# Routed experts on one core: gate and up products of the next tile of places ahead of the down product of this one

## The chip, the cores and the metric

The kernel runs on one core of one Trainium2 chip. The metric is the device time of one execution in microseconds, and the median over the runs is compared. A core has five engines that work side by side, each on its own queue of instructions: TensorE (PE, with its weight loads shown as PEld), VectorE (DVE), ScalarE (ACT), GpSimd (POOL) and SyncE (SP). Here SP only issues loads and stores. POOL issues the scatters and computes small things.

## The reference

The input is x of 32 x 256 x 128 floats, that is T = 8192 tokens of 128 numbers. Two layers follow one another, and each has the form x + s * silu(g). In layer 0, s is a two-layer transformer with rotary attention and g is a mixture of 64 small experts. In layer 1, s is a linear attention with 16 heads of 8 numbers, and g is the part that the change touches:

```python
    x = hidden_states.reshape(-1, h)
    shared_out = _swiglu(x, shared_gate_w, shared_up_w, shared_down_w)
    logits = x @ gate_w
    topk_ids = jnp.argmax(logits, axis=-1)
    topk_val = jnp.max(logits, axis=-1)
    scores = jax.nn.sigmoid(topk_val)[:, None]
    xs = x * scores
    ...
    g = _grouped_mm(sorted_x, routed_gate_w, tokens_per_expert)
    u = _grouped_mm(sorted_x, routed_up_w, tokens_per_expert)
    d = _grouped_mm(jax.nn.silu(g) * u, routed_down_w, tokens_per_expert)
```

Each token goes to one of 32 experts. The expert multiplies it by a gate matrix and an up matrix (128 x 256 each), takes silu(gate) * up, and multiplies the result by a down matrix (256 x 128). Everything is in float32.

## The kernel before, in words

One function, `recurrent_kernel`, does both layers. Its last third is layer 1, and only that matters here. A tile is 128 tokens (or places), and a group is GT = 4 tiles.

*Sending.* Tokens are sorted by expert without a sort: every expert owns a whole number of tiles of 128 places, 96 tiles (S1) in all, and every token has a place. `send()` (L858) scatters the token rows from `s_rows` into the DRAM buffer `xslot`, one indirect DMA of POOL per tile of tokens.

*Routed experts.* `routed()` (L959) walks over 24 groups of 4 tiles of places. For a group it loads `e_x` from `xslot` (L963, two buffers), transposes it on PE (L132, into a PSUM bank `ps_tr`), and copies it to `e_xt` on ACT (L973). DVE makes the destination rows `e_toi` from the last column of `e_x` (L969 to L971). Then, for each of the four tiles:

- SP reads the tile's expert from `widx` and loads its three weight matrices as `e_w` (L983, 384 KB, six buffers);
- PE multiplies four 128 x 128 pieces into one PSUM bank `ps_sc` (L986): the two halves of the gate and of the up product. This is "the gate/up product" below;
- ACT takes the Silu of the gate half into `e_hs` (L991, three buffers), and DVE multiplies it by the up half (L992);
- PE multiplies `e_hs` by the down matrix in two pieces (L995), into half of a PSUM bank `ps_mm` (two buffers, shared with other work). This is "the down product";
- ACT copies it to `e_ys` (L999), and POOL scatters `e_ys` to the rows of `back` (L1000).

*Linear attention.* `linear_attention(g)` (L873) works on 4 tiles of tokens at a time, for 16 groups. It is beside the routed experts until the last group. Its steps on PE are L877 (queries), L885 (norms of queries), L895 (keys and values), L924 (states), L936 (queries times states), a transpose of `l_o` (L132), and L952 (output). DVE has a long chain for it: L911, L915, L916 (a reciprocal), L917, and after L936 the steps L938, four pairs L109/L110 (mean and variance) and L116. Between the last two stands a chain on POOL (L111, L112, L114: `bn_rs`). ACT takes a square root in each group (L914), for which another function table is loaded, and the Silu table again after it.

*The finish.* `finish(g)` (L1011) loads `back`, adds the shared expert's part by two products with the identity (L1021, L1022), takes Silu, multiplies by the attention and adds x. It waits for the scatters.

*What sets the order.* The functions are Python generators: at each `yield` another one goes on (`run`, `rolling`), and this gives the order in which the instructions are written down. The tile framework then places them at build time: it gives each instruction the priority of its place, keeps a clock from a cost table for every engine, and takes from the ready instructions the first. So the order on an engine is close to the written one but not equal to it; the gate/up product of a later tile stands ahead of the down product of an earlier one wherever the planner found the latter not yet ready. On the chip every engine takes its queue in exactly the order so fixed, and waits on semaphores.

Of the kernel before, what the change touches and what calls it, by code (L numbers as in the profile page):

```python
# [16 lines left out]
F32 = mybir.dt.float32  # L17
I32 = mybir.dt.int32
U32 = mybir.dt.uint32
AF = mybir.ActivationFunctionType  # L20
ALU = mybir.AluOpType
# [4 lines left out]
P = 128  # L26
BATCH, SEQ, D = 32, 256, 128
T = BATCH * SEQ
NT = T // P
GT = 4  # L30
# [4 lines left out]
E1, F1 = 32, 256  # L35
# [25 lines left out]
def recurrent_kernel(ctx: ExitStack, tc: tile.TileContext, x, consts, small0, wsd, wgu, wd, small1, bias1, wr, out):  # L61
    nc = tc.nc
    vec, act, pool, pe, sp = nc.vector, nc.scalar, nc.gpsimd, nc.tensor, nc.sync
# [9 lines left out]
    def bank(tag="mm", bufs=2):  # L73
        return psum.tile([P, GW], F32, tag=tag, name=f"ps_{tag}", bufs=bufs)
# [6 lines left out]
    back = dram.tile([T + S1 * P, D], F32, name="back")  # L81
    moe1 = dram.tile([T, D], F32, name="moe1")

    def rows(ap, g):
        return ap[g * GW : (g + 1) * GW].rearrange("(t p) d -> p t d", p=P)
# [42 lines left out]
    def transposed(src):  # L128

        ps = bank("tr", 2)  # L130
        for j in range(GT):
            pe.transpose(ps[:, j * P : (j + 1) * P], src[:, j], ident)  # L132
        return ps
# [175 lines left out]
    with ExitStack() as c0:  # L309
# [3 lines left out]
        wk = c0.enter_context(tc.tile_pool(name="wk0", bufs=2, side="right"))  # L313
# [489 lines left out]
    wk = ctx.enter_context(tc.tile_pool(name="wk1", bufs=2))  # L803
# [20 lines left out]
    widx = w1p.tile([1, S1], I32, name="widx")  # L824
# [10 lines left out]
    owner = w1p.tile([S1, 1], F32, name="owner")  # L835
# [5 lines left out]
    ps = bank()  # L841
# [14 lines left out]
    sent, returned, last_norm = [], [], []  # L856
# [101 lines left out]

    def routed():  # L959

        for i in range(S1 // GT):
            xg = wk.tile([P, GT, D + 1], F32, name="e_x", bufs=2)
            ins = sp.dma_start(xg, rows(xslot, i))  # L963
            for d in sent[-8:]:
                tc.add_manual_dep(ins.ins, d.ins.name, waits, reason="reads what all the scatters wrote")
            ps = transposed(xg[:, :, :D])
            to = wk.tile([P, GT], F32, name="e_to")
            toi = wk.tile([P, GT], I32, name="e_toi", bufs=6)
            vec.tensor_scalar(to, xg[:, :, D], 0.0, None, ALU.is_equal)  # L969
            vec.tensor_tensor(to, to, spare[:, i * GT : (i + 1) * GT], ALU.mult)  # L970
            vec.scalar_tensor_tensor(toi, to, -1.0, xg[:, :, D], ALU.add, ALU.add)  # L971
            xt = works[1].tile([P, GW], F32, tag="chan", name="e_xt")
            act.copy(xt, ps)  # L973
            ys = works[1].tile([P, GT, D], F32, tag="out", name="e_ys")
            yield
            for j in range(GT):
                wt = wk.tile([P, 3 * F1], F32, name="e_w", bufs=6)
                at = i * GT + j
                row = nc.values_load(
                    widx[:, at : at + 1], engines={mybir.EngineType.SP}, min_val=0, max_val=(E1 - 1) * P,  # L980
                    skip_runtime_bounds_check_because="the owner is held at E1 - 1",
                )
                sp.dma_start(wt, wr[bass.ds(row, P)])  # L983
                ps = bank("sc", 4)
                for c in range(4):
                    pe.matmul(  # L986
                        ps[:, c * P : (c + 1) * P], wt[:, c * P : (c + 1) * P], xt[:, j * P : (j + 1) * P],
                        start=True, stop=True,
                    )
                hs = wk.tile([P, F1], F32, name="e_hs", bufs=3)  # L990
                act.activation(hs, ps[:, :F1], AF.Silu)  # L991
                vec.tensor_tensor(hs, hs, ps[:, F1:], ALU.mult)  # L992
                yp = bank()
                for c in range(2):
                    pe.matmul(  # L995
                        yp[:, :D], hs[:, c * P : (c + 1) * P], wt[:, 2 * F1 + c * D : 2 * F1 + (c + 1) * D],
                        start=c == 0, stop=c == 1,
                    )
                act.copy(ys[:, j], yp[:, :D])  # L999
                ins = pool.indirect_dma_start(  # L1000
                    out=back, out_offset=bass.IndirectOffsetOnAxis(ap=toi[:, j : j + 1], axis=0),
                    in_=ys[:, j], in_offset=None,
                )

                if returned:
                    tc.declare_no_dep(ins.ins, group="returned", reason="the rows are disjoint")
                tc.add_to_no_dep_group("returned", ins.ins)
                returned.append(ins)
                yield

    def finish(g):  # L1011

        tl = slice(g * GT, (g + 1) * GT)
        tag = ("gate", "tok", "chan", "out")[g % 4]
        gr = work(g // 4 + g).tile([P, GT, D], F32, tag=tag, name="f_g")
        ins = sp.dma_start(gr, rows(back, g))
        for d in returned[-8:]:
            tc.add_manual_dep(ins.ins, d.ins.name, waits, reason="reads what all the scatters wrote")

        ps = bank("sc", 4)  # L1020
        pe.matmul(ps, ident, xt_at[g], start=True, stop=False)  # L1021
        pe.matmul(ps, ident, gr.rearrange("p t d -> p (t d)"), start=False, stop=True)  # L1022
        act.activation(gr, ps.rearrange("p (t d) -> p t d", d=D), AF.Silu)
        yield
        vec.tensor_tensor(gr, gr, s_all[:, tl], ALU.mult)
        vec.tensor_tensor(gr, gr, x_at[g], ALU.add)
        sp.dma_start(rows(out, g), gr)
        yield

    sending, routing = send(), routed()  # L1030
    attending = rolling([linear_attention(g) for g in range(NG - 1)], 3)
    while len(sent) < NT:
# [94 lines left out]
```

## Time and profile before

| what | value |
|---|---|
| median of 3 runs | 1350.44 us (1348.21 to 1351.1) |
| the profiled execution | 1348.85 us |
| its span, first to last instruction | 1347.1 us |
| PE busy over the span | 1226.4 us (91%) |
| DVE, ACT, POOL busy | 940.0, 785.7, 650.4 us |
| mean granted clock of PE | 0.972 |
| gate/up products (L986), first and last start | 1050.6 and 1299.8 us |
| down products (L995), first and last start | 1054.9 and 1301.6 us |

A row of the profile's groups or of its timeline names engine, line, operation, the tile written and the tiles read. A float32 product of 128 columns shows as two passes, so one tile's gate/up product is x8 and its down product x4. A bracket such as `[0.74 <-DVE e_hs L992]` says how long the engine stood still before that row and whose end released it. A matmul's end is modelled: rows overlap, and eight passes advance PE by 0.89 us where each is shown longer.

### The profile page before, as it was taken

What the parts mean: (1) busy time and instruction counts of PE and PEld (TensorE: products, weight loads), DVE (VectorE), ACT (ScalarE), POOL (GpSimd) and SP (SyncE); (2) the same over time, 40 slices, a digit from 0 to 9 for tenths busy, and PEclk for the clock granted to TensorE, in tenths of its full rate; (3) what the DMA queues carried; (4) which work ended last, traced back from release to release, by engine and by line L of the source; (5) the groups of instructions that cost most, each with busy time, mean ns of one, the idle gap of its engine ahead of it and who ended that gap; (6) DMA issues with size and microseconds to landing.
All of it is one profiled execution on the core that took longest, in us unless ns stands there. A gap on an engine that the chain in (4) does not pass through costs nothing. (4 is left out here: it accounts for less than half of the span.)

```text
span 1347.1 us, 22826 instructions
## 1 busy us (share of the span) xinstructions
PE 1226.4 (91%) x7425; PEld 864.0 (64%) x7425; DVE 940.0 (70%) x3064; ACT 785.7 (58%) x1858; POOL 650.4 (48%) x1020
## 2 busy tenths in 40 slices
PE   6989999999999799999997978899999899999797
PEld 4547576576566477667665645566566778788773
DVE  4699779879879746655664866667767666666437
ACT  1785665675676576766775766353545555545342
POOL 6362822732721656665736365442677243443440
PEclk9999999999999999999998988889989899999999
DMA  5020301301302232223201142411211556666667
GB/s 181 22 55 25 118 17 47 118 25 40 102 25 81 69 81 55 57 57 74 59 7 39 42 116 63 124 32 55 93 44 46 172 185 209 203 200 199 185 210 201
DMA packets 135079, 125.80 MB, mean 93 GB/s; under 512 B 17104, under 2 KB 110256, under 8 KB 134832
## 3 DMA queue, kind: packets, MB, share of 16 engines
q1 hardware_dynamic: 123696, 108.57, 27.0%
q0 software_dynamic: 11264, 15.78, 4.8%
q8 instruction: 59, 0.97, 0.3%
q14 instruction: 60, 0.49, 0.1%
HBM read 83.63 MB, written 40.68 MB: 92 GB/s over the span
## 5 line engine op out<-in xcount | busy, mean ns | idle before, releaser
L1000 POOL DMA_INDIRECT back<-e_ys,e_toi x96 | 96.3, 1003 | 129.3 <-ACT e_ys L999 104.5
L601 ACT ACTIVATE a_pr<-ps_sc,a_nm 128x256 f32<-128x256 f32 x256 | 119.1, 478 | 59.2 <-DVE a_nm L592 59.1
L663 PE MATMUL ps_mm<-xt,sw 128*128 128x512 f32 x256 | 134.1, 630 | 1.6 <-ACT e_y L523 0.9
L111 POOL TENSOR_SCALAR bn_rs<-bn_mv 128x4 f32<-128x4 f32 x112 | 28.7, 256 | 218.5 <-DVE bn_mv L110 191.1
L125 POOL TENSOR_SCALAR z<-s_rows,bn_rs 128x128 f32<-128x128 f32 x256 | 128.4, 521 | 6.6
L681 PE MATMUL ps_mm<-sw,m_h 128*128 128x128 f32 x1024 | 127.9, 279 | 2.3 <-ACT e_y L523 1.3
L681 PEld LDWEIGHTS ps_mm<-sw,m_h 128*128 128x128 f32 x1024 | 119.6, 192 | 12.8 <-issue 6.0
L668 DVE SCALAR_TENSOR_TENSOR m_h<-m_h,m_z 128x512 f32<-128x512 f32 x128 | 89.5, 703 | 46.0 <-ACT m_h L667 45.3
L112 POOL TENSOR_TENSOR bn_rs<-bn_rs,power 128x4 f32<-128x4 f32 x112 | 116.7, 1043 | 1.3
L592 DVE TENSOR_REDUCE a_nm<-ps_sc 128x2 f32<-128x512 f32 x128 | 83.3, 679 | 31.9 <-PE ps_sc L586 31.7
L986 PE MATMUL ps_sc<-e_xt,e_w 128*128 128x128 f32 x768 | 101.4, 278 | 2.9 <-ACT e_xt L973 2.9
L665 ACT ACTIVATE m_z<-ps_mm,fold 128x512 f32<-128x512 f32 x128 | 87.3, 685 | 28.3 <-PE ps_mm L663 27.9
L986 PEld LDWEIGHTS ps_sc<-e_xt,e_w 128*128 128x128 f32 x768 | 94.3, 194 | 9.3 <-ACT e_xt L973 4.9
L586 PE MATMUL ps_sc<-a_qk,a_qk 64*128 64x256 f32 x512 | 96.7, 412 | 1.2 <-ACT a_pr L601 1.1
L524 POOL DMA_INDIRECT sums<-e_y,sidx x32 | 51.1, 1598 | 80.5 <-ACT e_y L523 39.5
L618 PE MATMUL ps_tr<-con,a_pr 128*128 128x128 f32 x512 | 75.9, 278 | 9.4 <-ACT a_pt L619 5.5
L618 PEld LDWEIGHTS ps_tr<-con,a_pr 128*128 128x128 f32 x512 | 59.3, 143 | 37.8 <-issue 19.3
L667 ACT ACTIVATE m_h<-m_z 128x512 f32<-128x512 f32 x128 | 80.8, 635 | 1.7
L860 POOL DMA_INDIRECT xslot<-s_rows,dest x64 | 68.3, 1067 | 24.1 <-issue 18.5
L619 ACT COPY a_pt<-ps_tr 128x512 f32<-128x512 f32 x128 | 71.7, 590 | 12.8 <-PE ps_tr L618 11.7
L558 PE MATMUL ps_mm<-xt,sw 128*128 128x512 f32 x128 | 69.0, 645 | 6.5 <-ACT xt L546 2.7
L627 PE MATMUL ps_mm<-a_pt,a_v 128*64 128x256 f32 x512 | 70.9, 396 | 4.2 <-ACT m_z L665 3.5
(236 smaller groups left out, 2951.1 us busy)
## 6 DMA issues: line engine op xcount, KB each, us to landing
e_w<-in_wr_dram SPq DMA_DIRECT2D x96, 384.0 KB, 3.8
xslot<-zero SPq DMA_DIRECT2D x4, 1548.0 KB, 7.0
e_x<-xslot SPq DMA_DIRECT2D x24, 258.0 KB, 4.0
e_wg<-in_wgu_dram SPq DMA_DIRECT2D x16, 384.0 KB, 3.2
x_in<-in_x_dram SPq DMA_DIRECT2D x16, 256.0 KB, 3.7
tab<-s_rows SPq DMA_DIRECT2D x16, 256.0 KB, 2.4
sums<-s_y SPq DMA_DIRECT2D x16, 256.0 KB, 2.3
sums<-zero SPq DMA_DIRECT2D x4, 1024.0 KB, 8.4
```

What stands on the lines that cost most here:

```text
L112: pool.tensor_tensor(rs[:, 0], rs[:, 0], power, ALU.pow)
L125: ins = pool.tensor_scalar(dst[:, j], src[:, j], rs[:, 1, j : j + 1], rs[:, 0, j : j + 1], ALU.add, ALU.mult)
L586: pe.matmul(sc[h][:, j * SEQ : (j + 1) * SEQ], qk[0][hd, q0 : q0 + P], qk[1][hd, b * SEQ : (b + 1) * SEQ], start=True, stop=True,)
L592: vec.tensor_reduce(nm[:, 2 * h : 2 * h + 2], sc[h].rearrange("p (j k) -> p j k", k=SEQ), AX.X, ALU.max, negate=True)
L601: act.activation(pr[:, n], sc[h][:, j * SEQ : (j + 1) * SEQ], AF.Exp, bias=nm[:, n : n + 1], accum_out=su[:, n : n + 1],)
L618: pe.transpose(pts[:, n * P : (n + 1) * P], pr[:, n, k * P : (k + 1) * P], ident)
L663: pe.matmul(ps, par("w1", l * FF0 + f * P, P), xt, start=True, stop=True)
L665: act.activation(z, ps, AF.Identity, bias=fold[:, l, 3 + f : 4 + f])
L668: vec.scalar_tensor_tensor(h, h, 1.0, z, ALU.add, ALU.mult)
L681: pe.matmul(ps[:, j * D : (j + 1) * D], hs[f][:, j * P : (j + 1) * P], par("w2", l * FF0 + f * D, D), start=f == 0, stop=f == 3,)
L986: pe.matmul(ps[:, c * P : (c + 1) * P], wt[:, c * P : (c + 1) * P], xt[:, j * P : (j + 1) * P], start=True, stop=True,)
L1000: ins = pool.indirect_dma_start(out=back, out_offset=bass.IndirectOffsetOnAxis(ap=toi[:, j : j + 1], axis=0), in_=ys[:, j], in_offset=None,)
```

## The change

The body of the tile loop is split into two functions. `widened` loads the weights, multiplies gate and up, and takes silu and product; `returns` multiplies by the down matrix, copies and scatters. The loop calls `widened` for a tile and then `returns` for the tile before it, across the border of a group too. After the last tile `returns` is called once more. The operations and their counts are the same; only the place of `returns` in the written order moves by one tile.

```diff
+        def widened(at, xt):
+            wt = wk.tile([P, 3 * F1], F32, name="e_w", bufs=6)
...
+            sp.dma_start(wt, wr[bass.ds(row, P)])
+            ps = bank("sc", 4)
+            for c in range(4):
+                pe.matmul(ps[:, c * P : (c + 1) * P], wt[:, c * P : (c + 1) * P], xt, start=True, stop=True)
+            hs = wk.tile([P, F1], F32, name="e_hs", bufs=3)
+            act.activation(hs, ps[:, :F1], AF.Silu)
+            vec.tensor_tensor(hs, hs, ps[:, F1:], ALU.mult)
+            return wt, hs
+
+        def returns(wt, hs, ys, to):
+            yp = bank()
+            for c in range(2):
+                pe.matmul(
+                    yp[:, :D], hs[:, c * P : (c + 1) * P], wt[:, 2 * F1 + c * D : 2 * F1 + (c + 1) * D],
+                    start=c == 0, stop=c == 1,
+                )
+            act.copy(ys, yp[:, :D])
+            ins = pool.indirect_dma_start(
+                out=back, out_offset=bass.IndirectOffsetOnAxis(ap=to, axis=0), in_=ys, in_offset=None,
+            )
...
+        behind = None
         for i in range(S1 // GT):
...
             for j in range(GT):
-                wt = wk.tile([P, 3 * F1], F32, name="e_w", bufs=6)
-                at = i * GT + j
...
-                hs = wk.tile([P, F1], F32, name="e_hs", bufs=3)
-                act.activation(hs, ps[:, :F1], AF.Silu)
-                vec.tensor_tensor(hs, hs, ps[:, F1:], ALU.mult)
-                yp = bank()
...
-                yield
+                ahead = widened(i * GT + j, xt[:, j * P : (j + 1) * P])
+                if behind:
+                    returns(*behind)
+                behind = (*ahead, ys[:, j], toi[:, j : j + 1])
+                yield
+        returns(*behind)
+        yield
```

In the built programs, with the planner's order, both kernels have the same work on every engine: the same products on PE, and the same 34 loads of a function table on ACT. Lines of the changed kernel are numbered differently: the gate/up product is L972 there, Silu L974, the product with the up half L975, the down product L982, the copy L986, the scatter L987, the weight load L969, and for a group L999 (load of `e_x`), L1005 to L1007 (destinations) and L1009 (copy to `e_xt`).

More of the change, by code (lines that the diff above doesn't have):

```diff
@@ L959, in routed @@
     def routed():
+        def widened(at, xt):
+            wt = wk.tile([P, 3 * F1], F32, name="e_w", bufs=6)
+            row = nc.values_load(
+                widx[:, at : at + 1], engines={mybir.EngineType.SP}, min_val=0, max_val=(E1 - 1) * P,
+                skip_runtime_bounds_check_because="the owner is held at E1 - 1",
+            )
[17 more added lines that the diff above has]
+                out=back, out_offset=bass.IndirectOffsetOnAxis(ap=to, axis=0), in_=ys, in_offset=None,
+            )
+            if returned:
+                tc.declare_no_dep(ins.ins, group="returned", reason="the rows are disjoint")
+            tc.add_to_no_dep_group("returned", ins.ins)
+            returned.append(ins)
+        behind = None
         for i in range(S1 // GT):
@@ L976, in routed @@
             for j in range(GT):
-                wt = wk.tile([P, 3 * F1], F32, name="e_w", bufs=6)
-                at = i * GT + j
[L979 to L989, printed above, removed]
-                hs = wk.tile([P, F1], F32, name="e_hs", bufs=3)
-                act.activation(hs, ps[:, :F1], AF.Silu)
-                vec.tensor_tensor(hs, hs, ps[:, F1:], ALU.mult)
-                yp = bank()
[L994 to L1008, printed above, removed]
+                ahead = widened(i * GT + j, xt[:, j * P : (j + 1) * P])
+                if behind:
+                    returns(*behind)
+                behind = (*ahead, ys[:, j], toi[:, j : j + 1])
                 yield
+        returns(*behind)
+        yield
     def finish(g):
```

## The prediction

> **What bounds the kernel now.** I read first the slices of the page, then a table of stretches, to find the stage that the change touches and what fills it. It runs from the first gate/up product (1050.6 us) to the last down product (1301.6 us).
>
> ```profile
> PE   6989999999999799999997978899999899999797
> ...
> sum 253.00, PE 234.25 PEld 204.92 DVE 146.36 ACT 129.22 POOL 109.85; mean PE 46.85 PEld 40.98 DVE 29.27 ACT 25.84 POOL 21.97
> ```
>
> The sum is over 1050 to 1303 us. PE is busy for 234.25 of 253 us and no other engine for over 147. The change takes no work from PE, so what can be won is at most PE's idle time, 253 - 234.25 = 18.75 us, 1.4% of the whole. The second view is the waits of that stretch (waiting instruction, releaser, us in total, times, longest), those of PE and two of DVE:
>
> ```profile
> DVE e_hs L992 <- ACT e_hs L991: 40.6, 42, 2.6
> ...
> DVE e_to L969 <- DMA e_x<-xslot: 12.3, 12, 2.2
> ...
> PE ps_mm L995 <- DVE e_hs L992: 9.6, 15, 1.6
> ...
> PE ps_tr L132 <- DVE l_o L116: 4.8, 2, 2.7
> ...
> PE ps_sc L986 <- ACT e_xt L973: 2.9, 5, 1.5
> ...
> PE ps_mm L995 <- DVE l_n L888: 1.0, 2, 0.5
> ```
>
> PE's four make 18.3 us, so they are the whole idle time. Half of it, 9.6 us, is what the change goes for: the down product waits for its `e_hs`. The third view, the timeline, shows why it waits where the wait is long:
>
> ```profile
> 1097.57 1.28 ACT L991 ACT_TABLE_LOAD   x1
> 1097.72 0.17 DVE L969 TENSOR_SCALAR e_to<-e_x 128x4 f32<-128x4 f32 x1 [1.13 <-DMA e_x<-xslot]
> 1098.86 0.95 ACT L991 ACTIVATE e_hs<-ps_sc 128x256 f32<-128x256 f32 x3
> 1099.97 1.35 DVE L916 RECIPROCAL l_n<-l_n 128x192 f32<-128x192 f32 x1
> 1101.23 1.02 DVE L992 TENSOR_TENSOR e_hs<-e_hs,ps_sc 128x256 f32<-128x256 f32 x3
> 1101.65 1.16 PE L995 MATMUL ps_mm<-e_w,e_hs 128*128 128x128 f32 x8 [1.36 <-DVE e_hs L992]
> ```
>
> The first Silu was done at about 1099.2, but DVE took the product only at 1101.23: it had stood behind the load of `e_x` and then had the attention's chain to do. So a long wait is DVE's queue, not the length of gate, silu, product, down.
>
> **The change part by part.** *Nothing is added or removed*: by the instruction order of the two built programs, both have 384 matmuls of gate/up, 192 of down, and 34 table loads. What moves is the down product with its copy and its scatter.
>
> *Cover.* I call cover the PE work that stands between the end of a tile's gate/up product and its down product, added up in each program's order with the advance per instruction that the timeline shows (0.223 us a 128 x 128 product, 0.112 a transpose, 0.86 a 512-wide one). The cover needed with nothing in the way is 1.11 us (gate/up advanced to 1109.46, down at 1110.57). Before, the median of the 96 tiles is 1.74 us and 10 are under 1.1; after, 2.68 us and 3. The planner had already put a later gate/up product ahead nearly everywhere. What 1.11 us lacks sums to 2.2 us before and 0.3 after: that is the certain part, 1.9 us. In the last 16 tiles, without attention beside them, the cover goes only from 1.01-1.12 to 1.01-1.34.
>
> *The waits, place by place.* For the rest I walked the after order at each place where PE waits before, with durations from this trace (Silu 0.38, product 0.42, L916 1.26, four L109/L110 1.6, L116 0.3 for the first, POOL's chain 1.6 from L111 to the end of L114, `e_x` 4.2 from issue to landing).
>
> (a) `e_to` stands ahead of an `e_hs` on DVE and waits for `e_x`: 1143.10, 1154.93, 1165.94, 1287.62, waits 0.74 + 0.62 + 0.30 + 0.72 = 2.38. From the transposes that free the buffer to the down product behind, PE work is 4.17, 4.55, 4.84, 4.68; with the wait added, about 5.15 is needed. After: 4.84, 4.77, 5.73, 5.47, so 0.3 at the first; the second is reached late, through (d). 2.38 becomes 0.3.
>
> (b) The place above and its twin 1224.68 (1.36 + 1.55 = 2.91). After, the means L109/L110 go ahead of the wait for `e_x`, but L116 comes in before `e_hs`, and PE has 5.47 instead of 6.25 from freeing to down. Walk: issue and landing 4.25, L915 to L916 1.8, L116 0.5 (it waits for POOL), product 0.4: 7.0 against PE at 5.8. 2 x 1.2, and 0.15 each for `e_xt`: 2.7.
>
> (c) The groups of tiles 24 to 27 and 68 to 71 (waits at 1125.94, 1131.74 and 1250.11), where, after, L938 to L916 go ahead of the second `e_hs`: before 0.23 + 0.54 + 1.37 = 2.14. After, counted from the transposes of `e_x`: ACT is through root and second table load at 6.65 and through Silu at 7.0, DVE through L916 at 8.1 and the product at 8.5, and PE is there at 7.0: 1.6 twice, and 0.3 for L888: 3.5. A loss.
>
> (d) `e_xt`: 1149.57 (1.52), 1173.83 (0.66) and three of 0.20 to 0.24, 2.86. At the first, nothing lay between transposes and product before; after, 1.48 us does, and the 1.52 goes. But in the same group L916 (3.6 us after L936) goes ahead of an `e_hs` that PE wants at 2.8: 1.3. The others stay: 2.64.
>
> (e) `l_o` transposed: 2.67 + 2.12 = 4.79. At the first, POOL's `bn_rs` stood behind a scatter whose down product came late; after, that scatter is of tiles finished before L936, and the 2.67 goes. At the second, PE has 2.7 us of work from L936 to the transpose instead of 4.0, and the chain takes 4.9 with one scatter ahead: 2.3, and 0.5 behind it. 2.8.
>
> (f) Waits of 0.18 to 0.49: 1.66 before. After 0 but for a down product right behind L936 (0.5, twice): 1.0. The first wait (0.99) stands, the one for L888 at 1180.07 (0.49) falls to 0.2.
>
> Sum before 0.99 + 2.38 + 2.91 + 2.14 + 2.86 + 4.79 + 1.66 + 0.49 = 18.2. After 0.99 + 0.3 + 2.7 + 3.5 + 2.64 + 2.8 + 1.0 + 0.2 = 14.1. The walk goes only to places that wait before; a new order has others, for which I put 1.0 (four of the size of (f)). Gain 18.2 - 15.1 = 3.1 us. Its bounds: a gain of 18.3, all idle time, and a loss of 5.1, worked out under *slower*.
>
> *What else moves.* The copy and scatter follow the down product: copies wait 81.3 us in total on PE already, POOL is 43% busy here, and nobody needs a row of `back` before the finish. The last down product still comes right behind the last gate/up product, so the finish starts as before. The weight load of tile n+6 waits on SP for down product n. From there to its gate/up product is 4.24 us of PE work at least before and 5.13 after; issue to landing takes 3.8 us (median, 5.0 at most), and no gate/up product waits for weights before: no cost. `e_x` loads stand at the same place of SP's queue or at most two weight loads later.
>
> [...] The waits in (b), (c), (d) lie behind a pair of table loads. In the trace, table load to root to table load to Silu is 1095.89 to 1098.86, 2.97 us. [...] In the trace PE stood 1.36 us with ready products behind the waiting one: 3.1 stays.
>
> **The rivals.** *Nothing*: the planner had done it; the waits that remain are DVE's, and (c) and (d) give back what (a) and (e) win: 1350.4. For: the cover of 86 tiles was enough. Against: (e)'s 2.67 us hangs on one scatter's place.
>
> *All of it*: cover lets DVE be late everywhere: 9.6 us of `e_hs` and 1.0 of L888 go, (c) and (d) don't come: 1341. Against: at (b) cover is smaller after.
>
> *Slower*, by one mechanism: DVE's attention chain now goes ahead of `e_hs`, from L938 to L916 and in places L116. From L936 it takes about 4.0 us, and PE has 2.8 to 3.6 us of other work. Were this paid in all nine groups at 1.5 us, 13.5 us would stand against the 8 us that my sum has for such waits ((b), (c), 1.3 in (d), 1.0 in (f)): 5.5 more, 2.4 over the gain, 1352.8; and with 0.3 of L116 in each, 2.7 more, 1355.5. It decides from where `e_x` lands over 4.7 us after its issue (4.3 is the median here, 5.4 the longest) or POOL's `bn_rs` comes later than L916.
>
> **How the numbers follow.** 3.1 us off the span of 1347.1 gives 1344.0, the profiled execution 1345.7 instead of 1348.85; the median of the runs lies 1.6 us above that execution: 1347.3. Chances: this case 45% (own range 1344.5 to 1349.5), nothing 20%, slower 20%, all of it 15%. The range goes half into the last two: 1342 to 1353.5. 0.2%, 2.7 us, is about what these runs can tell apart (their spread is 2.9). Faster by more, below 1347.7: all of it and 27 of the 45: 0.42. Slower by more: 0.22. Between: 0.36.
>
> **What would show it.** Right: PE idle in this stage of about 15 us; waits of the down product on `e_hs` of about 7 us, with the longest at (c); no wait of 2.7 us on L116 near the 13th attention group, one of about 2.3 near the 14th; DVE's waits on `e_x` under 12.3. Wrong: gate/up waiting for `e_w`; down waits that appear in every group behind L916; a longer stretch from the last down product to the end.

## The result, and the profile after

The changed kernel takes 1337.55 us (median of 6 runs, 1331.24 to 1343.91) against 1351.36 us before (6 runs, 1348.21 to 1354.09). The ratio is 0.9895, with a 95% interval of 0.9877 to 0.9914: 13.8 us or 1.05% faster, where 3.1 us were forecast. It lies outside the range, below its low end of 1342.

The profiled execution took 1336.66 us. I split the span of both at the first gate/up product and at the last down product, by the starts of these rows:

| part, us | before | after | difference |
|---|---|---|---|
| before the stage | 1050.8 | 1053.9 | +3.1 |
| stage: first gate/up start to last down start | 250.9 | 237.1 | -13.8 |
| last down start to the end | 45.4 | 43.8 | -1.6 |
| span | 1347.1 | 1334.9 | -12.2 |

The gain lies in the stage. The part ahead of it is the same work in both kernels and still differs by 3.1 us between these two executions, so it is partly luck that the stage and the medians give the same 13.8 us. First the page of after (PE's 40 slices):

```profile
span 1334.9 us, 22827 instructions
...
PE   6989999999999899999998877889999899999997
```

Now the table of stretches, cut to the stage alone in each kernel. The columns are the length and the busy time of each engine.

```profile
sum 251.50, PE 232.75 PEld 204.41 DVE 145.66 ACT 129.18 POOL 109.05; mean PE 232.75 PEld 204.41 DVE 145.66 ACT 129.18 POOL 109.05
```
```profile
sum 237.90, PE 226.44 PEld 201.02 DVE 148.29 ACT 130.53 POOL 108.51; mean PE 226.44 PEld 201.02 DVE 148.29 ACT 130.53 POOL 108.51
```

PE's idle time falls from 18.75 to 11.46 us, 7.3 less. But its *busy* time falls too, by 6.3 us, although the products are the same in number and size and the granted clock was 0.99 and 1.00. A busy time that shrinks with no work taken away held something other than work.

So I counted anew, from start to start. In the trace the pass of a 128-column product begins 0.111 us after the one before it where nothing holds it (transposes 0.109, 512 columns 0.429). By these advances the stage has 216.3 us of PE work in both kernels. All beyond it is time by which matmuls start late: 34.6 us before, 20.8 us after. The rows hide the difference to the idle time, because a row of 128 columns is shown 0.275 us long and ends 0.164 us after the next could have begun.

| late time in the stage, us | before | after | difference |
|---|---|---|---|
| idle, as the rows show it | 18.75 | 11.46 | -7.3 |
| hidden in gaps over 0.2 us, behind the shown end of a matmul | 4.5 | 2.6 | -1.9 |
| gaps of up to 0.2 us, wholly hidden | 11.3 | 6.7 | -4.6 |
| sum | 34.6 | 20.8 | -13.8 |
| of it ahead of down products | 20.0 | 11.3 | -8.7 |
| ahead of gate/up products | 7.0 | 4.1 | -2.8 |
| ahead of transposes of `l_o` | 5.3 | 3.1 | -2.2 |

The waits of after, the answer to the list in the prediction (waiting instruction, releaser, us in total, times, longest):

```profile
DVE e_hs L975 <- ACT e_hs L974: 44.2, 54, 2.3
...
PE ps_mm L982 <- DVE e_hs L975: 6.9, 8, 1.1
...
DVE e_to L1005 <- DMA e_x<-xslot: 5.4, 6, 1.8
...
PE ps_tr L132 <- DVE l_o L116: 2.5, 3, 1.4
...
PE ps_tr L132 <- DMA e_x<-xslot: 1.0, 2, 0.8
...
PE ps_sc L972 <- ACT e_xt L1009: 0.6, 2, 0.4
```

Down products wait 6.9 us instead of 9.6, the layer norm's `l_o` costs 2.5 us instead of 4.8. DVE's wait for `e_x` falls from 12.3 to 5.4 us. New is 1.0 us of PE for `e_x` itself, near the end.

The timeline of after at the place that the prediction's third view showed:

```profile
1099.52 1.28 ACT L974 ACT_TABLE_LOAD   x1
...
1100.66 0.17 DVE L1005 TENSOR_SCALAR e_to<-e_x 128x4 f32<-128x4 f32 x1 [0.33 <-DMA e_x<-xslot]
...
1100.82 0.39 ACT L974 ACTIVATE e_hs<-ps_sc 128x256 f32<-128x256 f32 x1
...
1101.09 1.35 DVE L916 RECIPROCAL l_n<-l_n 128x192 f32<-128x192 f32 x1
...
1102.90 1.08 DVE L975 TENSOR_TENSOR e_hs<-e_hs,ps_sc 128x256 f32<-128x256 f32 x3
...
1103.13 0.30 PE L132 MATMUL ps_tr<-con,l_o 128*128 128x128 f32 x1 [0.53 <-DVE l_o L116]
...
1103.36 0.71 PE L982 MATMUL ps_mm<-e_w,e_hs 128*128 128x128 f32 x4
```

DVE still comes late to the product: the chain with L916 stands ahead of it as before. But PE has other work to do, and loses 0.53 us here instead of 1.36.

### The profile page after: what moved, and what is told of

The parts are those of the page before. It is cut to its first block, busy times and chain, and to the rows that moved or that the text cites. A ratio compares the mean times of both kernels' runs of the same rounds, so it can differ in the third digit from the quotient of the medians.

```text
span 1334.9 us, 22827 instructions
## 1 busy us (share of the span) xinstructions
PE 1222.2 (92%) x7425; PEld 863.2 (65%) x7425; DVE 943.5 (71%) x3064; ACT 787.6 (59%) x1858; POOL 650.6 (49%) x1020
## 5 line engine op out<-in xcount | busy, mean ns | idle before, releaser
L987 POOL DMA_INDIRECT back<-e_ys,e_toi x96 | 95.1, 991 | 106.3 <-ACT e_ys L986 73.2
L111 POOL TENSOR_SCALAR bn_rs<-bn_mv 128x4 f32<-128x4 f32 x112 | 27.9, 249 | 230.4 <-DVE bn_mv L110 207.0
L972 PE MATMUL ps_sc<-e_xt,e_w 128*128 128x128 f32 x768 | 100.8, 278 | 1.0 <-ACT e_xt L1009 0.6
L972 PEld LDWEIGHTS ps_sc<-e_xt,e_w 128*128 128x128 f32 x768 | 94.5, 194 | 9.8 <-issue 7.8
```

What stands on the lines that cost most here:

```text
L972: pe.matmul(ps[:, c * P : (c + 1) * P], wt[:, c * P : (c + 1) * P], xt, start=True, stop=True)
L987: ins = pool.indirect_dma_start(out=back, out_offset=bass.IndirectOffsetOnAxis(ap=to, axis=0), in_=ys, in_offset=None,)
```

## The experiments

Three theories were set against one another. *Theory 1*: PE loses the time at down products whose `e_hs` comes just in time or late, everywhere in the stage and half of it unseen in the rows; the cover takes it away. *Theory 2*: the gain comes from attention's chain, whose instructions the new order puts earlier on DVE and POOL. The steps from group to group spoke for it: from group 18 to 19 before took 17.8 us and after 10.6. *Theory 3*: the small gaps come from the weight load, since `e_hs` is the stationary operand and can't be loaded before it is finished.

Chips differ: the kernel before took 1349.4, 1366.3, 1367.0 and 1349.7 us on the four chips used here. Each result is therefore given as the ratio to runs of the kernel before on the same chip; stage times and late time come from the profiled execution of each.

### The down product without its wait

```diff
-                        yp[:, :D], hs[:, c * P : (c + 1) * P], wt[...],
+                        yp[:, :D], ident, wt[...],
```

> The kernel before, with one edit: the down product takes a constant tile as its stationary operand in place of e_hs, so its result is not the routed expert's. Silu and the multiply still run and write e_hs, but TensorE never waits for it; TensorE's passes are the same in number and size. Theory 1 (TensorE loses the time in many small waits for an e_hs that comes just in time, half of them hidden in the rows' busy time; counted from start to start of matmuls the down product's rows of before are 20.0 us late in sum): all of that goes, the stage from the first gate/up product to the last down product falls from 251 us to about 231 to 234 us, the time to 1330 to 1335 us. Theory 2 (the gain of the change came from attention's chain of VectorE and GpSimd being ordered earlier, and the waits for e_hs only stand where another wait would take over): the stage stays over 243 us, the time over 1344 us. Step as predicted (only 9.6 us of waits for e_hs can be won, and most of them come back elsewhere): 1341 to 1347 us.

Measured: 1329.99 us, ratio 0.9852 (0.9824 to 0.9879). The stage takes 232.2 us; down products are late by 4.0 us in sum instead of 20.0. The waits of PE in the stage:

```profile
PE ps_tr L132 <- DVE l_o L116: 4.2, 3, 2.5
PE ps_mm L995 <- DVE l_n L888: 1.2, 2, 0.6
PE ps_sc L895 <- DVE e_hs L992: 0.4, 1, 0.4
PE ps_sc L986 <- ACT e_xt L973: 0.4, 1, 0.4
```

This is what theory 1 said: what the waits for `e_hs` cost in the kernel before is about 19 us, not 9.6, and little comes back elsewhere. The late time of the whole stage falls from 34.6 to 16.7 us. PE's busy time in the stage is 226.5 us here, 6.3 less than before; up to 0.9 us of this is a 512-column product of the finish, which comes behind the last down product in this run. One caution: the planner knows of the missing wait and sets down products earlier, so this run isn't the old order without its waits. The change doesn't win a share of just this: ahead of down products it won 8.7 us where this run won 16.0, and it won 2.2 us ahead of the transposes of `l_o`, which are no better here (5.8 us late, 5.3 before).

### Half of the change

```diff
+                if i > 11 or (i == 11 and j == GT - 1):   # the second run: if i < 12
+                    returns(*behind)
+                    behind = None
```

> The change in groups 0 to 11 alone; in groups 12 to 23 each tile's down product follows its own gate/up product as before. Theory 1 (many small waits for e_hs, everywhere): the first twelve groups take about 127 us as in the changed kernel (133.8 before), the last twelve about 117 us as before; the time is 1343 to 1346 us. Theory 2 (attention's chain at one place, from group 18 to 19, where the changed kernel gained 7.1 us): no more than the first half's 6.4 us can show, and if it comes from attention's order rather than from the cover, it shows less than 3 us: 1347 to 1351 us.

> The change in groups 12 to 23 alone, the first twelve as before. Theory 1: the first twelve groups take about 134 us as before, the last twelve about 110 us as in the changed kernel (117.1 before), the time is 1342 to 1345 us, and what this and the run with the first half gain add up to the whole gain of 13 to 14 us. Theory 2 (one place, group 18 to 19): the step from group 18 to 19 takes 10 to 11 us instead of 17.8 and the time is 1338 to 1343 us, with all of the gain in that one group.

| us | ratio to before (95%) | groups 0 to 11 | groups 12 to 23 | late in group 18 |
|---|---|---|---|---|
| before | 1 | 133.8 | 117.1 | 7.2 |
| first half linked | 0.9951 (0.9933 to 0.9970) | 127.8 | 116.2 | 6.5 |
| second half linked | 0.9943 (0.9923 to 0.9963) | 136.2 | 110.8 | 0.4 |
| changed kernel | 0.9895 (0.9877 to 0.9914) | 127.4 | 109.7 | 0.5 |

By the ratios the halves gain 6.6 and 7.7 us, which add up to 14.3: the whole. Each half gains where it is linked. The order of the matmuls in groups 0 to 11 of the second run is that of before, and yet it took 136.2 us there instead of 133.8: one execution is good to some 2.4 us in a half, no better. Both theories hold a part. In the first half no transpose of `l_o` was late before, and the gain is spread: in the first run late time falls there from 15.8 to 9.9 us, by 4.0 ahead of down products and 2.8 ahead of gate/up products, and 0.9 is lost elsewhere. That is what cover would do; but attention's order changes with it, and no run parts the two there. In the second half nearly all of the gain stands in one group, 18.

### The change at one place

> The change in groups 16 to 19 alone, elsewhere as before. In group 18 matmuls are 7.2 us late in sum before and 0.5 us in the changed kernel, among them two waits for l_o (2.8 us in group 18, 2.3 us in group 19). Theory 2 for this place (one scatter less ahead of the layer norm's chain on GpSimd, one wait for l_o gone): 5 to 7 us, the time is 1342.5 to 1345 us and one of the two long waits for l_o is left. Theory 1 (cover alone, evenly in all groups): one sixth of the change's gain, 2.3 us, 1346.5 to 1348 us.

Measured: ratio 0.9945 (0.9928 to 0.9961), 7.5 us on a chip with 1366.34 us before. Group 18 is late by 0.4 us instead of 7.2, and one wait for `l_o` is left. In this profiled execution groups 16 to 19 are late by 7.0 us less than in the trace of before, but the other groups, which keep the old way, by 3.6 more; no trace of before was kept on this chip, so whether the chip or the execution does that is open. Theory 2 holds at this place, and the two timelines show how. POOL before, around the 13th attention group:

```profile
1251.37 1.85 POOL L1000 DMA_INDIRECT back<-e_ys,e_toi  x1 [2.32 <-ACT e_ys L999]
1253.53 0.96 POOL L1000 DMA_INDIRECT back<-e_ys,e_toi  x1 [0.30 <-issue]
1254.56 0.19 POOL L111 TENSOR_SCALAR bn_rs<-bn_mv 128x4 f32<-128x4 f32 x1
```

the last row of DVE that L111 needs:

```profile
1252.31 0.17 DVE L110 BATCH_NORM_AGGREGATE bn_mv<-bn_st 128x2 f32<-128x6 f32 x1
```

and PE in the same stretch:

```profile
1250.11 1.13 PE L995 MATMUL ps_mm<-e_w,e_hs 128*128 128x128 f32 x8 [1.37 <-DVE e_hs L992]
...
1256.59 0.58 PE L132 MATMUL ps_tr<-con,l_o 128*128 128x128 f32 x2 [2.67 <-DVE l_o L116]
```

The down product is late, so its copy and its scatter are; the scatter stands ahead of `bn_rs` in POOL's queue, so L111 starts 2.1 us after its input was finished (1252.48), the layer norm is late, and then PE is late again: one late `e_hs` is paid twice. After, on POOL:

```profile
1241.62 0.19 POOL L111 TENSOR_SCALAR bn_rs<-bn_mv 128x4 f32<-128x4 f32 x1 [1.96 <-DVE e_to L1006]
...
1243.72 1.05 POOL L987 DMA_INDIRECT back<-e_ys,e_toi  x1 [0.51 <-issue]
```

POOL had been idle when L111 came, and no scatter was ahead of it. Which of the two counts more, the place of the scatter or the earlier down product, the runs don't part.

### The operands exchanged

```diff
-                        yp[:, :D], hs[:, c * P : (c + 1) * P], wt[:, 2 * F1 + c * D : ...],
+                        yp[:, :D], wt[:, 2 * F1 + c * D : ...], hs[:, c * P : (c + 1) * P],
```

> The kernel before with the two operands of the down product exchanged: e_w is the stationary one, e_hs the moving one, so that each tile comes out transposed and the output is not the reference's; TensorE's order and the number and size of its passes are those of before. Theory 3 (the bubbles of 50 to 200 ns, 10.3 us in sum before, are the weight load of an e_hs that was finished so late that its load could not be pulled ahead of the pass before): bubbles of that size ahead of down products fall by at least half, and the time is 1342 to 1346 us. Theory 1 without it (the bubbles are e_hs itself being late): the time stays at 1349 to 1352 us.

Measured: ratio 1.0015 (1.0004 to 1.0026). The gaps of 50 to 200 ns sum to 10.31 us, before to 10.25. Theory 3 falls: which operand is late makes no difference. In the trace of before a weight load in the stage begins 0.109 us ahead of its own pass (median), 2 ns behind the start of the pass before it, and none begins ahead of that pass. What these gaps are is taken up in the last section: 4.7 us of the 10.25 stand at the second pass of a down product, and 3.4 more at passes of other products right behind a late one.

### Two tiles ahead

If cover is what counts, more of it should gain more. A second tile ahead needs a fourth buffer of `e_hs`, for which there is no room; the first try takes a buffer from `e_w`, and a control has the changed kernel with five.

```diff
-                if behind:
-                    returns(*behind)
-                behind = (*ahead, ys[:, j], toi[:, j : j + 1])
+                if len(behind) > 1:
+                    returns(*behind.pop(0))
+                behind.append((*ahead, ys[:, j], toi[:, j : j + 1]))
```

> The changed kernel with 5 buffers for e_w instead of 6, the order of TensorE's matmuls being the same; it is the control for the run that goes two tiles ahead, which needs the room. Theory 1 (waits for e_hs set the gain; weights come early enough, no gate/up product waited long for e_w): as the changed kernel, a ratio to before of 0.988 to 0.992, 1335 to 1339 us. If weights are near the limit, gate/up products wait for e_w and the time is 1341 us or more.

> Gate and up of two tiles of places ahead of the down product, with 4 buffers for e_hs and 5 for e_w. By the order of its matmuls no tile has less than 1.5 us of TensorE work between its gate/up product and its down product (18 in the changed kernel, 30 before), and 71 of 96 have over 3 us (44, 25). Theory 1 (cover, and with it both the waits for e_hs and the bubble of 0.08 to 0.10 us behind each): of the 11.3 us that down products are late in the changed kernel 7 to 9 go, the stage takes 228 to 231 us, the time is 1328 to 1332 us, close to that of the kernel whose down product does not wait at all (1330). Theory 2 (attention's chain on VectorE and GpSimd, ordered earlier, gave the gain): no more than 2 us better than the control, 1334 to 1339 us. If the loads of weights become the limit: 1340 us or more.

Measured: the control 0.9841 (0.9811 to 0.9871), so five buffers cost nothing that shows; two ahead 0.9935 (0.9908 to 0.9962). Theory 1's forecast fails here, though its mechanism shows: down products are late by 7.2 us instead of the control's 12.3, but gate/up products by 18.0 instead of 4.5. PE's waits in the run two ahead:

```profile
PE ps_sc L972 <- DMA e_w<-in_wr_dram: 7.4, 9, 1.5
...
PE ps_mm L982 <- DVE e_hs L975: 2.4, 4, 1.0
```

A tile that waits for its down product keeps its `e_w`, whose down matrix is still wanted. With two such tiles and five buffers the loads had too little lead here: the 7.4 us above. So I took the room elsewhere, from `l_st` (one buffer instead of two), and ran the changed kernel again on the same chip.

> The changed kernel again, for a ratio on the same chip as the run that goes two tiles ahead: 0.987 to 0.992 of the time of before by both theories.

> Gate and up two tiles ahead of the down product with 6 buffers for e_w and 4 for e_hs; the room comes from l_st, which has one buffer instead of two. No tile has under 1.5 us of TensorE work between gate/up and down. In the run with 5 buffers down products were 5 us less late than in its control, but gate/up products 13.5 us later, most of it waiting for e_w. If the sixth buffer cures that (a buffer is held two tiles longer, not the loads being slow): gate/up products are late by under 8 us in sum, down products by 5 to 7 us, the stage takes 230 to 235 us, and the ratio to before is 0.981 to 0.986. If l_st with one buffer holds the attention up, or the loads themselves are the limit: the stage stays over 237 us and the ratio over 0.990.

Measured: the changed kernel 0.9857 (0.9832 to 0.9882), two ahead 0.9888 (0.9866 to 0.9911). Like the control above, the changed kernel does better on this slower chip than was expected: it wins 19.5 us, where it won 13.8 on the chip of the result. Its stage is as long on both, and no trace of before was kept here, so where the rest comes from is open. The waits for `e_w` are gone and gate/up products are late by 5.4 us, so the buffers were the cause of that. But the forecast fails again: the stage takes 240.0 us instead of 230 to 235, and down products are late by 11.3 us instead of 5 to 7. The first twelve groups take 125.1 us, the same as without any wait for `e_hs` (124.9). The last twelve take 114.9 instead of the changed kernel's 108.8: the last transpose of `l_o` is late by 2.7 us in group 19, and in groups 21 to 23, which have no attention beside them, single down products are late by 2.1, 0.5 and 0.7 us. The last two runs part the end from the buffers:

```diff
-                if len(behind) > 1:
+                while len(behind) > (1 if i < 16 else 0):
```

> Two tiles ahead in groups 0 to 15, one ahead from group 16 on, with 6 buffers for e_w, 4 for e_hs and one for l_st. Going two ahead all through, the first twelve groups took 125.1 us (128.2 in the changed kernel on that chip, 124.9 where the down product did not wait for e_hs at all), but groups 19 to 23 were 4.6 us later than in the changed kernel. Theory 1 (cover, place by place): the first twelve groups take 125 to 126 us, the last twelve 109 to 111 us, the stage 234 to 236 us, and the ratio to before is 0.982 to 0.986, a little under the changed kernel's. If the loss at the end came from l_st's one buffer or from the buffers of e_hs, not from going two ahead there: the last twelve groups still take over 113 us, and the ratio is over 0.988.

> The changed kernel with one buffer for l_st instead of two, the order of TensorE's matmuls being the same; the control for the two runs that take their room from it. If that buffer is free: as the changed kernel, 0.985 to 0.991 of before, the stage at 236 to 239 us. If it holds attention up: the stage takes over 240 us, and waits behind l_st (the products of L936) show.

Measured: two ahead and then one 1333.89 us, 0.9883 (0.9861 to 0.9905), the control 1337.31 us, 0.9896 (0.9872 to 0.9921). In the profiled execution of the first the stage takes 234.1 us, 3.0 less than in the changed kernel, with 124.5 us for the first twelve groups and 109.6 for the last. With the same buffers, the loss in those traces goes when the end has one tile ahead; the ratios of the runs, 0.9888 and 0.9883, don't show it. The stage of the control took 241.3 us in its one profiled execution, longer than forecast, with 5.4 us late at `l_o` and `e_x` in the last half, but the products of L936 wait no more (0.2 us late in sum) and its ratio is that of the changed kernel. Where those 4 us of one execution come from is open, since the order of the matmuls is the same. The ratio of the mixed version is a little above what theory 1 gave, and its interval covers the changed kernel's. It may be better by some 3 us; the runs don't show it.

### A yield instead of a tile

```diff
                 vec.tensor_tensor(hs, hs, ps[:, F1:], ALU.mult)
+                yield
                 yp = bank()
```

> The kernel before with one more yield between the multiply that makes e_hs and the down product, so that the planner may set attention's steps between the two, with no gate/up product of the next tile put ahead by the program. By the order of its matmuls 45 tiles have less than 1.2 us of TensorE work between gate/up and down (23 before, 3 in the changed kernel). Theory 1 (cover): about 20 more tiles pay the bubble of 0.08 to 0.10 us behind their wait and some wait longer, 2 to 5 us more than before: 1351.5 to 1355 us. If any new order of attention beside the experts brings the gain (a placebo): under 1345 us.

Measured: ratio 1.0078 (1.0047 to 1.0109), slower by 10.6 us. The sign is that of theory 1, and a new order alone is no gain. The size is not its: down products are late by 26.8 us (20.0 before), but gate/up products by 16.3 too (7.0). With one yield more per tile, attention takes more of its steps per tile: each of the first eleven groups of tiles holds 10.6 to 15.3 us of PE work and each of the last thirteen 4.4 to 7.1. So this run moved more than the cover and measures no price.

## Why the prediction was wrong

The sign and the mechanism were right. The step that failed is the base of the sum: "PE's four make 18.3 us, so they are the whole idle time", with "so what can be won is at most PE's idle time". That took the rows' busy time as fixed work, and put what is hidden in it at nothing. The cap of 18.75 us was not passed, but it was no cap. Counted from start to start, 34.6 us were lost, and 15.8 of them stood in the rows as busy. This hidden part gave 6.5 of the 13.8 us, and no place of the walk had any of it. It is also why the rival "all of it" gave 1341 for 9.6 us of waits: taking the wait for `e_hs` away altogether gave 1330.

The other 7.3 us are idle time, of which 18.2 - 15.1 = 3.1 were forecast, so the walk was mis-sized as well. Its old places came out 6.9 us too dear, (b), (c) and (e) by 1.4 to 1.6 us each, and its new places 3.2 us too cheap; that these offset in part is luck. The terms, in idle us as the rows of after show them:

| place | before | predicted after | measured after |
|---|---|---|---|
| first wait | 0.99 | 0.99 | 1.00 |
| (a) `e_to` waits for `e_x` | 2.38 | 0.3 | 0 |
| (b) DVE late behind `e_x` and L916 | 2.91 | 2.7 | 0.53 + 0.62 = 1.15 |
| (c) tiles 24 to 27, 68 to 71 | 2.14 | 3.5 | 0.99 + 0.99 = 1.98 |
| (d) `e_xt` | 2.86 | 2.64 | 1.15 + 0.36 + 0.23 = 1.74 |
| (e) transposes of `l_o` | 4.79 | 2.8 | 1.40 |
| (f) small waits | 1.66 | 1.0 | 0 |
| L888 | 0.49 | 0.2 | 0 |
| new | 0 | 1.0 | 1.06 + 1.06 + 2.08 = 4.20 |
| sum | 18.2 | 15.1 | 11.47 |

Five of these waits in after's timeline of PE, in order of time: a new one (its twin is left out), one of (c), the one of (d), the other of (c), and that of (e):

```profile
1083.04 0.71 PE L982 MATMUL ps_mm<-e_w,e_hs 128*128 128x128 f32 x4 [1.06 <-DVE e_hs L975]
...
1126.05 0.71 PE L982 MATMUL ps_mm<-e_w,e_hs 128*128 128x128 f32 x4 [0.99 <-DVE e_hs L975]
...
1148.93 0.71 PE L982 MATMUL ps_mm<-e_w,e_hs 128*128 128x128 f32 x4 [1.15 <-DVE e_hs L975]
...
1243.17 1.16 PE L982 MATMUL ps_mm<-e_w,e_hs 128*128 128x128 f32 x8 [0.99 <-DVE e_hs L975]
...
1258.26 0.33 PE L132 MATMUL ps_tr<-con,l_o 128*128 128x128 f32 x1 [1.40 <-DVE l_o L116]
```

- *Cover.* "The certain part" of 1.9 us was too small. The needed cover was taken at 1.11 us from a place with no idle time before the down product; but that row is 0.70 us long for four passes, and one that comes in good time is 0.61. In the kernel before all 15 tiles with 1.10 to 1.25 us from the last gate/up start to the down start and no wait before the first pass lose 0.08 us behind that pass. In after there are 3 such tiles.
- *(a)* came as predicted: DVE's wait for `e_x` no longer reaches PE.
- *(b)* was walked with `e_x` 4.25 us after its issue and all of DVE's chain behind it. In the trace `e_to` waited 0.33 us for `e_x` there, so DVE was free sooner. The walk's 1.2 us was 0.53 and 0.62. (It also sets PE at 5.8 us where it had counted 5.47, without a reason.)
- *(c)* and *(d)*: the loss ahead of `e_hs` behind L916 is there, at the very places, and 1.15 us at (d) is the forecast 1.3. At (c) it is 1.0 each and not 1.6. Of the waits for `e_xt`, the long one went and most of the small ones with it.
- *(e)* was right in its cause: the wait of 2.67 us went, and POOL's queue shows why. The second is 1.40 us instead of the 2.3 and 0.5 that I gave it. The two down products of 0.49 and 0.27 us beside it, counted under (f), went too.
- *(f)* and *new*: the two down products right behind L936 show no idle time. What came instead are two waits of 1.06 us, at 1083.04 and its twin 1200.06: on DVE four L116, which had waited for POOL's `bn_rs`, and L917 (1.22 us) stand ahead of `e_hs` there. The other 2.08 us are five waits of 0.25 to 0.77 us in the last four groups, for `e_x`, `e_hs` and `e_w`. For new places I had put down 1.0.
- *Slower* didn't come: its mechanism is there, the chain from L938 to L916 ahead of `e_hs` at three places ((c) and (d)) and L116 at two, but these cost 0.99 to 1.15 us each, 5.3 in all, where nine groups at 1.5 us were needed.
- *What else moves*: weights came in time but for one wait of 0.44 us, and the finish didn't move later. The run with two tiles and five buffers shows the price once the lead shrinks.
- *Table loads and order.* Table load, root, table load and Silu took 2.97 us in the trace of before and again at (b) (1097.85 to 1100.82), and the places behind such a pair came out at 1.15 us in (b), 1.98 in (c) and 1.15 in (d), below the 2.7, 3.5 and 1.3 of the walk. And the order was kept: the 7425 matmuls of each trace stand, line by line, in the order of the built queue, and PE stood 1.40 us at 1258.26 with a gate/up product behind the waiting transpose.

The signs that I named: idle of about 15 us (11.5), waits on `e_hs` of about 7 (6.9), the longest at (c) (it was at (d)), no wait of 2.7 us for `l_o` at the 13th attention group (none), one of about 2.3 at the 14th (1.40), DVE's wait for `e_x` under 12.3 (5.4).

## What to carry to other kernels

Where one engine sets the end and its queue is kept in order, count its lost time from start to start of its rows, against the shortest steady advance (0.111 us for a pass of 128 columns here): idle time in the profile was only half of what was lost here, 18.75 of 34.6 us. A product that is "just in time" wasn't free here (0.08 us a tile); put enough other work between a producer's chain and its consumer that the consumer's semaphore is up before the queue gets to it, and look whether the queue of another engine passes a delay on, as POOL's did here (1.37 us at a down product, then 2.67 at a transpose). One tile ahead cost no buffers. The second held its weights for longer (7.4 us of waits for `e_w` with five buffers), and where the neighbouring work ran out it cost more than it gave (114.9 us instead of 108.8 in the last twelve groups, with six).

## What was not expected of the hardware

In these traces a wait cost more than itself, by 0.08 to 0.10 us. Here are three down products of before from the timeline of PE: two that waited, and one that didn't.

```profile
1263.59 0.71 PE L995 MATMUL ps_mm<-e_w,e_hs 128*128 128x128 f32 x4 [0.49 <-DVE e_hs L992]
...
1267.48 0.71 PE L995 MATMUL ps_mm<-e_w,e_hs 128*128 128x128 f32 x4 [0.27 <-DVE e_hs L992]
...
1268.47 0.61 PE L995 MATMUL ps_mm<-e_w,e_hs 128*128 128x128 f32 x4
```

Here in the same kernel are two that show no wait and are nearly as long. DVE had finished their `e_hs` only 0.07 and 0.08 us before they began:

```profile
1110.57 0.70 PE L995 MATMUL ps_mm<-e_w,e_hs 128*128 128x128 f32 x4
...
1112.44 0.69 PE L995 MATMUL ps_mm<-e_w,e_hs 128*128 128x128 f32 x4
```

Four passes with nothing in the way are shown as 3 x 0.111 + 0.275 = 0.61 us. The other 0.08 to 0.10 us lies between the first and the second pass. It follows in all 27 tiles of before whose first pass was late by more than 0.05 us. 35 tiles began less than 0.1 us after the end of their `e_hs`, and all of them have it; of the tiles without it none began sooner than 0.14 us after. The number of tiles with it, and its sum, is:

| kernel | tiles of 96 | us |
|---|---|---|
| before | 51 | 4.7 |
| before, operands exchanged | 51 | 4.7 |
| changed kernel | 25 | 2.2 |
| down product without its wait | 17 | 1.6 |

So it goes with a release that comes just before the product, not with the operand. Of the 51 tiles of before, `e_hs` came within 0.15 us in 38, and another release (the read of L888 or a copy to `e_ys`) in six. Six more stand right behind the 16-column products of L885, with `e_hs` finished 1.1 to 4.2 us earlier, and one fits neither kind; what holds these seven no run shows, nor what fills the 0.08 to 0.10 us. What the trace does show is the weight load of the first pass: it begins 2 ns ahead of its pass in the 51 tiles and 109 ns ahead in the other 45 (medians).

In the changed kernel the chips differ outside this stage: it had 1053.9 us ahead of the stage on one chip and 1066.8 on another, and 237.1 and 236.9 us in it.
